# A GATv2 layer on one core: destinations loaded as 96 rows and 15, and the last destinations of units copied on chip

## The chip, the cores and the metric

The kernel runs on one core of a Trainium2 chip. The metric is the device time of one execution in microseconds (us). Three runs of the kernel before the change took 4048.72 to 4051.7 us, with a median of 4050.42.

## What is computed

One graph layer over 12500 nodes of 128 features and 400000 edges, which are sorted by destination. After a layer norm and a ReLU, the layer attends over the incoming edges of every node (GATv2, 8 heads of 16 features), and a feed-forward block follows:

```python
h = jnp.maximum(_layernorm(x, axis=-1), 0.0)
x = x + _L0_gnn_ref(h, edge_index, edge_attr_32, ...)

# within the layer
x_l = (x @ W_l).reshape(n, H, C)
x_r = (x @ W_r).reshape(n, H, C)
e = (ea @ W_e).reshape(-1, H, C)
m = jax.nn.leaky_relu(x_l[src] + x_r[dst] + e, NEG_SLOPE)
alpha = jnp.einsum('ehc,hc->eh', m, att)
a = softmax of alpha over the edges of each dst
out = jax.ops.segment_sum(x_l[src] * a[:, :, None], dst, num_segments=n)
...
h = x + _gatv2(_ln(x, ln1_g, ln1_b), edge_index, edge_attr, ...)
ff = jax.nn.gelu(_ln(h, ln2_g, ln2_b) @ W1 + b1, approximate=False) @ W2 + b2
return h + ff
```

## The kernel before

**Two parts.** A first part (the prologue, in `tile_gnn`) works on nodes: it loads x, computes layer norms and `x_l`, and stores `x_l` rows in DRAM (`xl_dram`). Then the main loop (`window_edges`) walks over the edges in 782 pairs of units; a unit is U = 256 edges. For each pair, GpSimd (POOL) issues four indirect DMAs of 128 rows each (`gather`, line 896), which fetch `x_l[src]` into a tile `xs`. `gather` runs four pairs ahead of PE's first use, and `xs` has 12 buffers. PE then combines, scores, transposes and sums; ACT and VectorE (DVE) work between its steps. The last nodes' softmax and feed-forward follow.

**The order in the prologue is written out by hand** (`tc.manual_schedule()`): each engine, and each DMA queue, executes its part in program order. Two queues matter here: SyncE's (SP), which issues the ordinary loads and stores, and GpSimd's, which issues the indirect loads. First all loads are issued: the node tiles (`load_x`), the destinations (`load_dst`), the constants (`load_consts`). Then 35 rounds follow. In each round every stage of `node_stages` handles one group of four node tiles, later stages working on earlier groups. Within a round, raw gathers and raw stores come first, then the one-time steps of certain rounds (`weights` in round 3, `edge_constants` in 7, `from_first` in 12, `fits` in 14), then the node stages. The stage `x_l` (line 535 stores its rows on SyncE's queue) starts in round 8.

**The raw batches.** 24 of the later pairs do not gather from `xl_dram`. Their four gathers are made during the prologue, straight from x (`raw_gather`, line 270), and are stored to DRAM three rounds later on SyncE's queue (`raw_store`, line 278). The tile `raw` has five buffers, so the sixth batch's gathers can begin only when the first batch has been stored.

**The destinations.** `load_dst` fills two tiles. `dc` holds all destinations, one row of EP = RU * U = 14 * 256 = 3584 edges in each of RP = 112 partitions, with the first U + 1 of the next row repeated behind it; places without an edge hold NO_NODE. Line 290 loads rows 0 to 110 as one DMA, line 293 and line 298 what is repeated behind the rows, line 302 row 111. `lu` holds the last destination of each of the 14 units of a row; it is loaded from DRAM at a stride of 256 elements (lines 305 and 308). The last unit with edges is only partly filled; line 314 puts the destination of the last real edge in its place. `from_first` casts `dc` to float (`df`, line 389) and computes, on GpSimd (`dlb`, line 393), the distance of each destination from the first of its unit or pair; `fits` reads `lu` and checks that the units suit the windowed path, and its flag chooses between `window_edges` and a general path.

`edge_constants` (first operation that needs a loaded constant: line 358, from `we_sb`) is VectorE's work in round 7. `load_consts` stands behind `load_dst` on SyncE's queue: lines 244 to 252, with `src_sb` (1568 KB, line 251) and `first_sb` (1568 single elements, line 252) as its last.

The order of the prologue:

```python
        load_x(0, min(GN, NT))
        load_raw()
        ...
        load_dst()
        load_consts()
        ...
        for r in range(max(max(len(qs), 9) + LAST + 1, rows_at[-1] + 4)):
            for d, at in zip(raw, rows_at):
                if r == at:
                    raw_gather(d)
                if r == at + 3:
                    raw_store(d)
```

Of the kernel before, what the change touches and what calls it, by code (L numbers as in the profile page):

```python
# [32 lines left out]
NO_NODE = 1 << 20  # L33
KU = 2
U = KU * P
UP = 2
QP = 4
RU = 14
# [5 lines left out]
XW = P + H  # L44
CX = XW // H
GN = 4
SPARE = 8
AHEAD = 4
WAHEAD = 3
# [41 lines left out]
def group_range(nc, pool, v, step, n):  # L91

    below = pool.tile([P, n], F32, name=f"below{n}")
    nc.vector.tensor_scalar(below, v, float(step), None, op0=OP.is_lt)
    nc.vector.scalar_tensor_tensor(v, v, 0.0, below, op0=OP.is_ge, op1=OP.mult)


def node_groups(nt):

    first = nt % GN  # L100
    return ([(0, first)] if first else []) + [(t, GN) for t in range(first, nt, GN)]


def edges_per_node(nt, n_edges):
    return -(-n_edges // (nt * P))


def done_after(nt, n_edges):

    return [-(-(t + n) * P * edges_per_node(nt, n_edges) // U) + SPARE for t, n in node_groups(nt)]  # L110


def xr_round(t0, nt, n_edges):

    first = (t0 * P - CW) * edges_per_node(nt, n_edges) // U - SPARE
    return first // UP - WAHEAD - XR_STEPS - 1


def raw_pairs(nt, n_edges):

    n_pr = -(-n_edges // (UP * U))
    at = [xr_round(t, nt, n_edges) + XR_STEPS + 1 for t in range(GN, nt, GN)]
    return [(r + RAW_STEPS + AHEAD + 1, r) for r in at if r + RAW_STEPS + AHEAD + 2 < n_pr]


def heads_of(nc, pool, out, att_c, fh):

    nc.vector.tensor_scalar(fh, fh, 0.0, None, op0=OP.is_equal)
    of = pool.tile([P, H], F32, name="of")
    nc.vector.tensor_reduce(of, fh, AX.X, OP.max)  # L130
    nc.vector.tensor_scalar(out, of, att_c, None, op0=OP.mult)
# [3 lines left out]
def tile_gnn(  # L135
# [23 lines left out]
    nc = tc.nc  # L159
# [6 lines left out]
    NUE = -(-n_edges // U)  # L166
    NU = -(-NUE // (UP * QP)) * UP * QP
    RP = -(-NU // RU)
# [23 lines left out]
    flag = keep.tile([1, 1], I32, name="flag")  # L192
    quads = [(t, min(GN, NT - t)) for t in range(0, NT, GN)]
    VAR = 6
    roots_sb = keep.tile([P, len(quads) + VAR, 2, GN], F32, name="roots_sb")
    mean_sb = keep.tile([P, NT], F32, name="mean_sb")
# [33 lines left out]
    EP = RU * U  # L230
    rest = NCH * CE - (RP - 1) * EP
    dc = rng.tile([RP, EP + U + 1], I32, name="dc")
    lu = rng.tile([RP, RU], I32, name="lu")

    def load_weights():
        nc.scalar.dma_start(wl_sb, w_l)
        nc.scalar.dma_start(wr_sb, w_r)
        nc.scalar.dma_start(g1_c, column(ln1_g))
        nc.scalar.dma_start(b1n_c, column(ln1_b))
# [40 lines left out]
    def load_x(t0, n):  # L280
        if n > 0:
            nc.sync.dma_start(h_sb[:, t0 : t0 + n, :], x_t[:, t0 : t0 + n, :])  # L282

    def load_dst():
        nc.gpsimd.memset(dc[:, EP : EP + U + 1], NO_NODE)
        if rest < EP:
            nc.gpsimd.memset(dc[(RP - 1) // DE * DE :, rest:EP], NO_NODE)
        if RP > 1:
            over = min(EP + U + 1, NCH * CE - (RP - 2) * EP)
            nc.sync.dma_start(  # L290
                dc[0 : RP - 1, 0:EP], bass.AP(tensor=dst.tensor, offset=dst.offset, ap=[[EP, RP - 1], [1, EP]])
            )
            nc.sync.dma_start(
                dc[RP - 2 : RP - 1, EP:over],
                bass.AP(tensor=dst.tensor, offset=dst.offset + (RP - 1) * EP, ap=[[0, 1], [1, over - EP]]),
            )
            if RP > 2:
                nc.sync.dma_start(
                    dc[0 : RP - 2, EP : EP + U + 1],
                    bass.AP(tensor=dst.tensor, offset=dst.offset + EP, ap=[[EP, RP - 2], [1, U + 1]]),  # L300
                )
        nc.sync.dma_start(dc[RP - 1 : RP, 0:rest], dst[(RP - 1) * EP :].rearrange("(o e) -> o e", o=1))
        nc.gpsimd.memset(lu, NO_NODE)
        if RP > 1:
            nc.sync.dma_start(
                lu[0 : RP - 1, :], bass.AP(tensor=dst.tensor, offset=dst.offset + U - 1, ap=[[EP, RP - 1], [U, RU]])
            )
        nc.sync.dma_start(
            lu[RP - 1 : RP, 0 : rest // U],
            bass.AP(tensor=dst.tensor, offset=dst.offset + (RP - 1) * EP + U - 1, ap=[[0, 1], [U, rest // U]]),  # L310
        )

        u = NUE - 1
        nc.sync.dma_start(
            lu[u // RU : u // RU + 1, u % RU : u % RU + 1],
            bass.AP(tensor=dst.tensor, offset=dst.offset + n_edges - 1, ap=[[0, 1], [1, 1]]),
        )


    def weights():  # L320
# [5 lines left out]
        wl_f = wl_c.rearrange("p c h -> p (c h)")  # L326
        ps = once_ps.tile([P, GN * P], F32, name="w_ps")
        nc.tensor.matmul(ps[:, 0:P], mean, wl_f, start=True, stop=True)
# [27 lines left out]
    def edge_constants():  # L356
        nc.vector.tensor_copy(ident_b, ident)
        nc.vector.tensor_copy(
            wer.rearrange("p (c h) -> p c h", h=H), we_sb.rearrange("p (h c) -> p c h", c=C)
        )  # L360
        heads_of(nc, build, attbd, att_c, fh)
        nc.vector.tensor_scalar(
            negrep, attbd[:, None, :].to_broadcast([P, NW, H]), -1.0, None, op0=OP.mult
        )
        nc.vector.tensor_scalar(nh, nh, 0.0, None, op0=OP.is_equal)
        mine = build.tile([P, H], F32, name="mine")
        nc.vector.tensor_reduce(mine, nh, AX.X, OP.max)
        nc.vector.tensor_copy(diag, mine[:, None, :].to_broadcast([P, CX, H]))
        nc.vector.tensor_scalar(own, own, 0.0, None, op0=OP.is_equal)
        nc.vector.tensor_scalar(last, last, 0.0, None, op0=OP.is_equal)  # L370
        nc.vector.tensor_sub(own, last, own)
        nc.vector.tensor_scalar(farw, own, BIG, None, op0=OP.mult)
        group_range(nc, build, third, NS, CW)
        nc.vector.tensor_mul(third, third, in_order)
        nc.vector.tensor_reduce(nid, third, AX.X, OP.add)
        nc.vector.tensor_scalar(unit, unit, 0.0, None, op0=OP.max)
        nc.vector.tensor_add(nid, nid, unit)
        nc.vector.tensor_scalar(fq, fq, 0.0, None, op0=OP.is_equal)
        qm = build.tile([P, QP], F32, name="qm")
        nc.vector.tensor_reduce(qm, fq, AX.X, OP.max)  # L380
        for q in range(QP):
            nc.vector.tensor_scalar(we_z[:, q, :], wer, qm[:, q : q + 1], None, op0=OP.mult)


    df = rng.tile([RP, EP + U + 1], F32, name="df")
    bad = rng.tile([RP, 2], F32, name="bad")

    def from_first():
        nc.vector.tensor_copy(df, dc)
# [11 lines left out]
    def fits():  # L401
# [30 lines left out]
        nc.vector.tensor_mul(place, place, place)  # L432
        nc.vector.tensor_scalar(off[:, 3], place, float(SPARE**2), None, op0=OP.is_gt)
        nc.vector.tensor_mul(off, off, real[:, None, :].to_broadcast([RP, 4, RU]))
# [270 lines left out]
    with tc.manual_schedule():  # L705
        make_identity(nc, ident)
        count_up()
        for t in xls:
            nc.gpsimd.memset(t[:, :, P:], 1.0)
        load_weights()  # L710
        load_x(0, min(GN, NT))
        load_raw()
        load_x(GN, min(3 * GN, NT - GN))
        for t in range(4 * GN, NT, 14):
            load_x(t, min(14, NT - t))
        load_dst()
        load_consts()
        nc.gpsimd.memset(empty, 0.0)
        nc.gpsimd.memset(empty[:, :, C + 1 : SH], CAP)
        rows_at = [i * 5 // 4 + (3 if i >= 10 else 0) for i in range(len(raw))]  # L720
# [6 lines that stand above are left out]
            if r == 3:  # L727
                weights()
            if r == 7:
                edge_constants()  # L730
            if r == 12:
                from_first()
            if r == 14:
                fits()
            for t in slots(r - 2):
                nc.vector.reciprocal(t, t)
            for t in slots(r - 1):
                nc.scalar.activation(t, t, AF.Sqrt)
            for late, f in node_stages:
                if 0 <= r - late < len(qs):  # L740
                    f(qs[r - late], r)
            if 0 <= r - LAST < len(first_xr):
                first_xr[r - LAST](qs[0])
        clear(0)
# [952 lines left out]
```

## Time and profile before

| | us |
|---|---|
| three runs: lowest, median, highest | 4048.72, 4050.42, 4051.7 |
| the profiled execution | 4055.89 |
| its span | 4053.7 |
| busy in the span: PE | 3555.2 (88%) |
| GpSimd (POOL) | 2984.9 (74%) |
| VectorE (DVE) | 2539.5 (63%) |
| ACT | 2135.2 (53%) |
| first and last gather of line 896 begin | 186.4 and 3981.5 |

The profile names an engine, a line of the kernel, and "out<-in" by tile names. A time "idle before" is that of the engine ahead of an instruction, with what ended it. SPq and POOLq are the engines' sequencers, which issue DMAs; the time of an issue on SPq includes what the queue waits for before it can hand the DMA on. In the chain of waits, "issue" is time in which an engine waited for nothing that the profile shows. The granted clock of PE was 0.955 over the span.

### The profile page before, as it was taken

What the parts mean: (1) busy time and instruction counts of PE and PEld (TensorE: products, weight loads), DVE (VectorE), ACT (ScalarE), POOL (GpSimd) and SP (SyncE); (2) the same over time, 40 slices, a digit from 0 to 9 for tenths busy, and PEclk for the clock granted to TensorE, in tenths of its full rate; (3) what the DMA queues carried; (4) which work ended last, traced back from release to release, by engine and by line L of the source; (5) the groups of instructions that cost most, each with busy time, mean ns of one, the idle gap of its engine ahead of it and who ended that gap; (6) DMA issues with size and microseconds to landing.
All of it is one profiled execution on the core that took longest, in us unless ns stands there. A gap on an engine that the chain in (4) does not pass through costs nothing.

```text
span 4053.7 us, 65778 instructions
## 1 busy us (share of the span) xinstructions
PE 3555.2 (88%) x19254; PEld 2501.5 (62%) x19255; DVE 2539.5 (63%) x5834; ACT 2135.2 (53%) x4638; POOL 2984.9 (74%) x3156
## 2 busy tenths in 40 slices
PE   2388888998989999999999999999989999989986
PEld 2356665665666666666666666666766666666664
DVE  5656665766666666666666666666666665666654
ACT  4544444544445555565455556555555555545543
POOL 4777777777777777777777777777777777777772
PEclk6699999999999999999999999999999999999998
DMA  5668878777766666656665665656666666565562
GB/s 160 198 165 198 185 194 197 171 163 165 172 124 126 126 124 131 123 121 129 132 125 124 128 129 120 136 123 117 124 136 126 124 130 128 107 135 114 120 134 50
DMA packets 648212, 560.85 MB, mean 138 GB/s; under 512 B 386387, under 2 KB 525506, under 8 KB 647602
## 3 DMA queue, kind: packets, MB, share of 16 engines
q1 hardware_dynamic: 547266, 339.01, 33.7%
q0 software_dynamic: 100000, 217.41, 30.2%
q8 instruction: 156, 2.56, 0.3%
q14 instruction: 214, 1.75, 0.2%
q10 hardware_dynamic: 576, 0.13, 0.0%
HBM read 489.81 MB, written 66.32 MB: 137 GB/s over the span
## 4 chain that ended last, share of the span: by engine, by line
PE 40%; POOL 24%; DMA 22%; issue 13%; SPq 1%; DVE 0%; ACT 0%; POOLq 0%; DVEq 0%; ACTq 0%
POOL xs L896 22%; DMA xs<-xl_dram,src_sb 21%; PE z L942 9%; PE acc L1000 8%; PE ab L960 7%; PE pt_ps L986 4%; PE z L938 4%; PE z L941 2%; PE ab L959 2%; POOL raw L270 2%; PE acc L1233 1%; PE acc L1208 1%; DMA lu<-in_dst 1%; SPq L282 0%; DMA state<-rec 0%
## 5 line engine op out<-in xcount | busy, mean ns | idle before, releaser
L896 POOL DMA_INDIRECT xs<-xl_dram,src_sb x3029 | 2873.0, 949 | 923.2 <-issue 796.0
L978 ACT ACTIVATE p<-ab,rec 128x256 f32<-128x256 f32 x1563 | 656.8, 472 | 1056.5 <-DVE rec L967 1044.3
L1009 DVE TENSOR_TENSOR own<-acc,diag 128x272 f32<-128x272 f32 x782 | 344.1, 440 | 1068.5 <-PE acc L1000 1039.6
L938 PE MATMUL z<-ident,xs 128*128 128x128 f32 x3125 | 573.3, 283 | 353.0 <-DMA xs<-xl_dram,src_sb 318.3
L938 PEld LDWEIGHTS z<-ident,xs 128*128 128x128 f32 x3125 | 399.5, 142 | 772.3 <-DMA xs<-xl_dram,src_sb 434.5
L1000 PE MATMUL acc<-xs,pt 128*128 128x136 f32 x6250 | 874.9, 284 | 0.2 <-DVE f_yo L1247 0.2
L942 PE MATMUL z<-ea,we_z 128*128 128x512 f32 x1564 | 835.4, 617 | 0.0
L1000 PEld LDWEIGHTS acc<-xs,pt 128*128 128x128 f32 x6250 | 802.6, 195 | 0.4 <-PE pt_ps L986 0.4
L960 PE MATMUL ab<-m,negrep 128*128 128x512 f32 x1564 | 801.4, 594 | 0.0
L991 ACT COPY pt<-pt_ps 128x512 f32<-128x512 f32 x782 | 455.9, 583 | 623.3 <-PE pt_ps L986 611.5
L986 PEld LDWEIGHTS pt_ps<-ident,p 128*128 128x128 f32 x3125 | 407.8, 146 | 438.2 <-issue 386.4
L967 DVE TENSOR_REDUCE rec<-ab 128x2 f32<-128x512 f32 x781 | 540.2, 692 | 123.4 <-PE ab L960 113.2
L953 DVE TENSOR_TENSOR m<-z,zs 128x512 f32<-128x512 f32 x782 | 533.0, 682 | 115.0 <-ACT zs L948 114.7
L948 ACT ACTIVATE zs<-z 128x512 f32<-128x512 f32 x782 | 472.2, 604 | 41.4 <-DMA dlw<-dc_dram 33.6
L986 PE MATMUL pt_ps<-ident,p 128*128 128x128 f32 x3125 | 489.2, 281 | 2.2 <-ACT pt L991 1.3
L1015 DVE TENSOR_REDUCE rec<-own 128x34 f32<-128x272 f32 x782 | 340.9, 436 | 26.7
L942 PEld LDWEIGHTS z<-ea,we_z 128*128 128x128 f32 x1564 | 306.5, 196 | 32.5
L960 PEld LDWEIGHTS ab<-m,negrep 128*128 128x128 f32 x1564 | 300.6, 192 | 37.1 <-issue 1.2
L941 PE MATMUL z<-ne,xrw 128*128 128x512 bf16 x782 | 304.0, 389 | 0.2 <-DMA xs<-xl_dram,src_sb 0.2
L959 PE MATMUL ab<-ne,farw 128*128 128x512 bf16 x782 | 299.6, 383 | 0.0
L924 DVE TENSOR_SCALAR ne<-dlw,nid 112x512 bf16<-112x512 bf16 x782 | 289.8, 371 | 13.0 <-DMA dlw<-du_dram 13.0
L270 POOL DMA_INDIRECT raw<-in_x,src_raw x96 | 95.5, 995 | 71.3 <-DMA raw_dram<-raw 40.1
(198 smaller groups left out, 2235.6 us busy)
## 6 DMA issues: line engine op xcount, KB each, us to landing
dlw<-dc_dram SPq DMA_DIRECT2D x196, 384.0 KB
ea<-in_ea_t SPq DMA_DIRECT2D x196, 256.0 KB
ea_s<-in_ea_t SPq DMA_DIRECT2D x98, 512.0 KB
xs<-xl_dram,src_sb POOLq DMA_INDIRECT x3029
state<-rec SPq DMA_DIRECT2D x1563, 9.0 KB
xrw<-xs_dram SPq DMA_DIRECT2D x782, 24.0 KB
state<-empty SPq DMA_DIRECT2D x28, 504.0 KB
st<-state SPq DMA_DIRECT2D x48, 288.0 KB
```

Of the source, the lines that this page charges most:

```text
L896: nc.gpsimd.indirect_dma_start(out=xs[:, j, :], out_offset=None, in_=xl_dram, in_offset=bass.IndirectOffsetOnAxis(ap=src_sb[:, c * KP + j ...
L938: nc.tensor.matmul(z[:, j * P : (j + 1) * P], d["xs"][:, j, 0:P], ident, start=(j == 0), stop=False, is_transpose=True)
L941: nc.tensor.matmul(z[:, :e], xrw[c % NV], d["ne"][:, :e], start=False, stop=False)
L942: nc.tensor.matmul(z[:, :e], we_z[:, c % QP, :], d["ea"][:, :e], start=False, stop=True)
L948: nc.scalar.activation(d["zs"][:, :e], d["z"][:, :e], AF.Copy, scale=SLOPE)
L953: nc.vector.tensor_tensor(d["m"][:, :e], d["z"][:, :e], d["zs"][:, :e], op=OP.max)
L960: nc.tensor.matmul(ab[:, :e], negrep.rearrange("p n h -> p (n h)"), d["m"][:, :e], start=False, stop=True)
L967: nc.vector.tensor_reduce(d["rec"][:, :, CX], d["ab"].rearrange("p (u e) -> p u e", e=U), AX.X, OP.min)
L978: nc.scalar.activation(d["p"][:, us], d["ab"][:, us], AF.Exp, bias=d["rec"][:, i, CX:SH], scale=-1.0)
L986: nc.tensor.transpose(d["pt_ps"][:, js], d["p"][:, js], ident)
L991: nc.scalar.copy(d["pt"][:, :e], d["pt_ps"][:, :e])
L1000: nc.tensor.matmul(d["acc"][:, i, :], d["pt"][:, j * P : (j + 1) * P], d["xs"][:, j, :], start=(j == js[0]), stop=(j == js[-1]),)
```

## The change

The load of rows 0 to 110 of `dc` is cut into two DMAs, of rows 0 to 95 and 96 to 110. The two strided loads of `lu` and its memset are removed. A new step, `last_of_units`, copies every 256th element of `dc` into `lu` on VectorE at the start of round 8, before that round's node stages; the single-element load into `lu` is moved behind this copy, and stands on SyncE's queue in round 8, behind that round's raw store and ahead of its `x_l` store.

```diff
+NQ = 16
...
         if RP > 1:
             over = min(EP + U + 1, NCH * CE - (RP - 2) * EP)
-            nc.sync.dma_start(
-                dc[0 : RP - 1, 0:EP], bass.AP(tensor=dst.tensor, offset=dst.offset, ap=[[EP, RP - 1], [1, EP]])
-            )
+            whole = (RP - 1) // NQ * NQ
+            for a, b in ((0, whole), (whole, RP - 1)):
+                if a < b:
+                    nc.sync.dma_start(
+                        dc[a:b, 0:EP],
+                        bass.AP(tensor=dst.tensor, offset=dst.offset + a * EP, ap=[[EP, b - a], [1, EP]]),
+                    )
...
-        nc.gpsimd.memset(lu, NO_NODE)
-        if RP > 1:
-            nc.sync.dma_start(
-                lu[0 : RP - 1, :], bass.AP(tensor=dst.tensor, offset=dst.offset + U - 1, ap=[[EP, RP - 1], [U, RU]])
-            )
-        nc.sync.dma_start(
-            lu[RP - 1 : RP, 0 : rest // U],
-            bass.AP(tensor=dst.tensor, offset=dst.offset + (RP - 1) * EP + U - 1, ap=[[0, 1], [U, rest // U]]),
-        )
-
-        u = NUE - 1
-        nc.sync.dma_start(
-            lu[u // RU : u // RU + 1, u % RU : u % RU + 1],
-            bass.AP(tensor=dst.tensor, offset=dst.offset + n_edges - 1, ap=[[0, 1], [1, 1]]),
-        )
...
+    def last_of_units():
+        nc.vector.tensor_copy(lu, dc[:, U - 1 : EP : U])
+
+        u = NUE - 1
+        nc.sync.dma_start(
+            lu[u // RU : u // RU + 1, u % RU : u % RU + 1],
+            bass.AP(tensor=dst.tensor, offset=dst.offset + n_edges - 1, ap=[[0, 1], [1, 1]]),
+        )
...
             if r == 7:
                 edge_constants()
+            if r == 8:
+                last_of_units()
```

## The prediction

> **What bounds the kernel now.** I read the page first, its chain and groups, then the indirect loads of line 896, then the first 200 us by engine, then SyncE's queue.
>
> ```profile
> L896 POOL DMA_INDIRECT xs<-xl_dram,src_sb x3029 | 2873.0, 949 | 923.2 <-issue 796.0
> ```
> ```profile
> L896 POOL DMA_INDIRECT xs<-xl_dram,src_sb x3029: 940/945/1702, 186.4 to 3981.5; - x190
>   issue: 796.0, 2611
>   DMA xs<-xl_dram,src_sb: 41.8, 137
> ```
> The first line is a group of the page, the others are the answer for line 896. (2873.0 + 923.2) / 3029 = 1.253 us from one gather to the next, and 3029 x 1.253 = 3796 us is the whole stretch from 186.4 to the last gather's end at 3982.5. The idle part is 0.30 us before every gather, whoever is named as releaser (41.8 / 137 = 0.305). So GpSimd never waits for a buffer in the main loop: it sets the pace, although PE is the busiest engine (88%). PE's wait for `xs` says the same from the other side, in the waits between 400 and 3900 us:
>
> ```profile
> PE z L938 <- DMA xs<-xl_dram,src_sb: 286.6, 290, 4.2
> ```
> The 71 us after the last gather (to 4053.7) drain the pipeline and the last nodes. What brings gather 1 forward thus brings the end forward one for one. GpSimd reaches it through 96 gathers of line 270, and these did wait: GpSimd's timeline,
>
> ```profile
> 30.41 0.94 POOL L270 DMA_INDIRECT raw<-in_x,src_raw  x1 [0.30 <-issue]
> 71.47 0.94 POOL L270 DMA_INDIRECT raw<-in_x,src_raw  x1 [40.12 <-DMA raw_dram<-raw]
> ```
> `raw` has 5 buffers of 4 gathers; the 21st waits until the first buffer has been stored. That store sits in SyncE's queue, whose timeline is:
>
> ```profile
> 20.25 2.83 SPq L290 DMA_DIRECT2D dc<-in_dst  x1
> ...
> 24.38 0.97 SPq L305 DMA_DIRECT2D lu<-in_dst  x1
> 25.40 25.56 SPq L308 DMA_DIRECT2D lu<-in_dst  x1
> 52.15 0.23 SPq L314 DMA_DIRECT2D lu<-in_dst  x1
> 52.43 0.38 SPq L244 DMA_DIRECT2D cols<-in_ln_g  x1
> ...
> 54.26 0.67 SPq L245 DMA_DIRECT2D cols<-in_att  x1
> 54.97 0.59 SPq L246 DMA_DIRECT2D we_sb<-in_w_e  x1
> ...
> 58.95 10.24 SPq L278 DMA_DIRECT2D raw_dram<-raw  x5
> ```
> The queue stands in L308 for 25.56 us. Why is told by the windows (PE, PEld, DVE, ACT, POOL busy, PE clock, DMA share, GB/s):
>
> ```profile
> 15.00:25.00 10.00, 3.75 (x14) 2.17 (x13) 7.70 (x47) 7.14 (x33) 7.56 (x9) 1.00 1.13 354
> 34.00:47.00 13.00, 0.00 (x0) 0.00 (x0) 0.00 (x0) 0.00 (x0) 0.00 (x0) 0.50 0.19 81
> ```
> While `h_sb` loads, all 16 DMA engines move 354 GB/s. From 34 to 47 us only `dc` moves: 0.19 x 16 = 3 engines, 81 GB/s, with every compute engine idle. Its 111 rows go to 3 engines (111 = 3 x 37; the trace has three landing events, 47.8 to 48.7). L305's 1554 single elements lie behind them on the same three (they land at 51.7), and L308 cannot be issued until they drain. VectorE stalls on the same delay, by its timeline:
>
> ```profile
> 57.20 0.27 DVE L358 COPY wer<-we_sb 128x128 f32<-128x128 f32 x1 [30.70 <-DMA we_sb<-in_w_e]
> ```
>
> **The change part by part.**
>
> *The dc load, split.* 96 = 16 x 6 rows and 15 = 15 x 1 rows, so 16 and 15 engines, by what the landing events show: rows are shared out evenly over a divisor of their number (111 rows, 3 events; the 110 rows of L298, 11). `h_sb` still comes first: its last landing events are at 25.9 to 27.3. The 1.59 MB of 111 rows at the 354 GB/s above take 4.5 us (gathers included in that rate, as they will be). From about 26.3 to 26.5 that gives 31.0 us for the 96 rows and 31.7 for the 15 (one row takes 0.54 us in the trace). Before: 48.7.
>
> [...] By the 0.19 row it gains 17 us, because the one transfer did not have 16 engines. [...]
>
> *The three lu loads, removed.* L305, L308 and L314 occupy SyncE from 24.38 to 52.38: 28.0 us including gaps. The split adds one issue (0.45, as the neighbour L293). Constants would then start at 52.43 - 28.0 + 0.45 = 24.9.
>
> *A wait that appears next.* In the trace each SyncE DMA names the semaphore that it waits for; eight are used in turn, so each DMA first waits for the landing of the one issued eight before. Before, L308 hid this. Counting after the change: the third L244 waits for the last `h_sb` (27.3), the fourth for the 96 rows (31.0), and L245 for the 15 rows (31.7). So L245 issues at 31.7, not 24.9 + 1.8 = 26.7. From L245 to the first raw store the order of issue is unchanged: 58.95 - 54.26 = 4.7 us. First raw store: 31.7 + 4.7 = 36.4, against 58.95, 22.5 us earlier. (The other eight-back DMAs, L293, L298 and L302, are small and land before 33; what waits for them issues later.)
>
> *From first store to gather 21.* 71.47 - 58.95 = 12.5 us: `src_sb` (1.6 MB) and the 1568 elements of `first_sb` lie ahead in the rings. Neither is touched and the rings are as empty at 35 us as they were at 57. Gather 21 starts at 36.4 + 12.5 = 48.9; the wait of 40.1 shrinks to 17.6. Gain 22.5 us.
>
> *VectorE.* `we_sb` is issued at 31.7 + 0.7 = 32.4 and landed 2.2 us after its issue (54.97, 57.2): 34.6, 22.6 earlier. VectorE and GpSimd move by the same amount, so what they do to each other later is kept: the gathers that took 2.5 and 3.8 us beside the cast of `df` and L404, and the 12.3 us of `dlb`.
>
> *The lu copy and the single-element load, added in round 8.* The nearest row is L410, 112x14 from int32, 0.17 us; by that row the copy costs 0.17, and a strided read could cost 0 to 0.4. VectorE is not GpSimd's limit. The one-element load takes SyncE 0.23 us, as L314 did. It waits for the copy, with the first xl store (L535) and then all later stores behind it. The copy is VectorE's first operation of round 8, at about 64.6 - 22.6 = 42; SyncE gets there after the fifth raw store, at 69.2 - 22.5 = 46.7. So it does not wait, and the xl store behind waits for later work of the same round anyway. If SyncE did get there first, the cost is bounded by slack: the raw stores land over 10 us before GpSimd wants their buffers (store 6 is issued at 78.7, gather 41 starts at 113.0). `fits` reads `lu` in round 14, 50 us on. Taken at nothing. A further DMA also shifts the turn of the semaphores by one; the xl store then waits for `src_sb`, which landed at 69.9, i.e. 47.3: 0.5 us, inside the same slack.
>
> *The removed memset of lu* (0.10 us on GpSimd) ran before GpSimd waited 2.66 us for `src_raw`: nothing.
>
> *Sum.* 22.5 us off GpSimd's start of the main loop, carried to the end. The profiled execution took 4055.89 us (span 4053.7, 2.2 outside it): 4033.4. It stands 5.5 above the median of 4050.42; the same 22.5 off the median gives 4027.9.
>
> Bounds of the unknown terms: if the rings hold `dc` up less, or the eight-back wait bites less, up to 5.0 more (27.5); if the slower gathers beside VectorE (1.5 and 2.8 us extra) fall elsewhere, 4 more; if `dc` at 16 engines runs at 250 GB/s, L245 comes 1.9 us later; if `src_sb` and `first_sb` meet traffic that they didn't meet before, up to 2.5 less.
>
> **The rivals.**
>
> 1. *No hold from the eight-back wait.* Constants run through from 24.9, gain 27.5: 4022.9. For it: L244 to L246 issue without a visible wait before. Against: their waits were over by then, and the semaphores are named in the records. 0.13.
>
> 2. [...] 0.05.
>
> 3. *PE is the true limit,* its backlog is merely hidden by 12 buffers, and an earlier start gives no earlier end: 4050. For it: PE is busy 92 of 100 us in the loop. Against: 286.6 us of waiting for `xs`, and no gather that waits for PE. 0.04.
>
> 4. *Slower: SyncE held by the new one-element load.* In round 8 it stands ahead of every xl and raw store. If the copy came late, the raw stores would come late, and GpSimd would wait at gather 41 (113.0 before, 90.4 after). It costs something only if SyncE is held beyond about 80 us, and the change loses only if held beyond about 103 (113.0 less the 10 us that the stores behind it need); each us from there is a us on the end, 4060 if held to 113. The copy needs only `dc` (31.7) and VectorE's round 7, so it is 60 us away from that point. 0.03.
>
> **How the numbers follow.** The main case has 0.75: 4027.9, by itself 4024 to 4032. The range of 4020 to 4033 takes in rival 1 with part of the 4 us of gathers; outside stay rivals 2, 3 and 4 (0.12) and some 0.07 at both ends. A measurement of this kernel can tell about 0.2% from no change, 8.1 us, so faster means below 4042.3: main case and rival 1, 0.88. Within: rivals 2 and 3, 0.09. Slower: rival 4, 0.03.
>
> **What would show each step.** GB/s near 350 up to 31 us and no window with 3 busy engines: the split. No issue of 25 us in SyncE's queue, and a hold of some 5 us at the fourth L244: the eight-back wait (if none, rival 1). VectorE's idle time before L358 about 8 us instead of 30.7; GpSimd's before gather 21 about 17.6 instead of 40.1. First gather of line 896 at 163.9 instead of 186.4, and 1.253 us apart as before. The forecast is wrong if `dc` still lands after 45, if gather 21 waits for something new, or if the 3029 gathers start to wait for PE.

## The result, and the profile after

| | before, us | after, us |
|---|---|---|
| median of 5 runs each, one chip | 4050.84 | 4033.17 |
| lowest to highest | 4048.72 to 4053.25 | 4031.16 to 4034.54 |
| the profiled execution (span) | 4055.89 (4053.7) | 4031.16 (4029.0) |
| gather 21 of the raw batches begins | 71.47 | 53.41 |
| first gather of the main loop begins | 186.38 | 168.53 |

The ratio is 0.9956, with a 95% interval of 0.9945 to 0.9967: 17.7 us less, where 22.5 were forecast. The predicted time was 4027.9, the range 4020 to 4033; the median lies 0.2 us above the range's upper end.

Lines 244 to 252 of before are lines 245 to 253 here, line 278 is 279 and line 896 is 897. The main loop runs as it did. The first line is the page's group, the others are the answer for line 897:

```profile
L897 POOL DMA_INDIRECT xs<-xl_dram,src_sb x3029 | 2868.9, 947 | 923.3 <-issue 792.7
```
```profile
L897 POOL DMA_INDIRECT xs<-xl_dram,src_sb x3029: 940/944/1554, 168.5 to 3959.6; - x190
  issue: 792.7, 2600
  DMA xs<-xl_dram,src_sb: 43.3, 142
```

(2868.9 + 923.3) / 3029 = 1.252 us from gather to gather, and still none of them waits for a buffer. What has moved is the start, by 186.38 - 168.53 = 17.85 us. The reason is at gather 21, in GpSimd's timeline (idle time before it in brackets):

```profile
30.22 0.94 POOL L271 DMA_INDIRECT raw<-in_x,src_raw  x1 [0.30 <-issue]
...
53.41 0.94 POOL L271 DMA_INDIRECT raw<-in_x,src_raw  x1 [22.25 <-DMA raw_dram<-raw]
```

It waited 22.25 us instead of 40.12. The queue that it waits for, SyncE's timeline (start, us, line):

```profile
20.16 3.93 SPq L294 DMA_DIRECT2D dc<-in_dst  x2
...
25.52 0.51 SPq L245 DMA_DIRECT2D cols<-in_ln_b  x1
27.70 7.53 SPq L245 DMA_DIRECT2D cols<-in_b  x2
36.28 0.70 SPq L246 DMA_DIRECT2D cols<-in_att  x1
37.02 0.58 SPq L247 DMA_DIRECT2D we_sb<-in_w_e  x1
...
41.02 10.47 SPq L279 DMA_DIRECT2D raw_dram<-raw  x5
51.61 0.76 SPq L382 DMA_DIRECT2D lu<-in_dst  x1
```

The 25.56 us in which the queue stood at a `lu` load are gone. In their place it stands at the third and fourth column (27.70 to 35.23) and at `att` (36.28). What it stands for is told by the waits of SyncE between 20 and 60 us (us in total, times, longest):

```profile
SPq L245 <- DMA dc<-in_dst: 6.9, 1, 6.9
SPq L245 <- DMA h_sb<-in_x: 1.7, 1, 1.7
SPq L246 <- DMA dc<-in_dst: 1.0, 1, 1.0
```

The fourth column waits for the 96 rows, `att` for the 15: each waits for the DMA issued eight before it. The last landing events of the 96 rows are at 34.9 us and of the 15 at 36.3, where 31.0 and 31.7 were forecast. The windows show how the time goes (PE, PEld, DVE, ACT, POOL busy, PE clock, DMA share, GB/s):

```profile
15.00:25.00 10.00, 3.80 (x14) 2.23 (x13) 7.77 (x48) 7.20 (x33) 7.55 (x8) 1.00 1.14 356
25.00:31.00 6.00, 4.56 (x22) 4.26 (x20) 1.31 (x6) 6.00 (x30) 4.56 (x5) 1.00 1.10 285
31.00:36.00 5.00, 1.55 (x12) 1.36 (x12) 0.00 (x0) 0.69 (x3) 0.16 (x1) 1.00 0.92 142
```

In none of these windows are only 3 DMA engines busy: the share is 0.92 and above. But from 31 to 36 us, with the DMA engines 92% busy, they move 142 GB/s. An engine can be busy with a row and move it slowly. In the DMA records, a 14336-byte row of `dc` took 536 ns in the median before, on its three engines; here it takes 986. A 12544-byte row of `src_sb`, 128 of them, takes 469. The raw gathers beside `dc` take longer too: between 25.5 and 35.5 us their 4096-byte rows take 296 ns in the median, where they took 167 before.

### The profile page after: what moved, and what is told of

Same layout as the page of the kernel before. It is cut to its first block, busy times and chain, and to the rows that moved or that the text cites. A ratio compares the mean times of both kernels' runs of the same rounds, so it can differ in the third digit from the quotient of the medians.

```text
span 4029.0 us, 65580 instructions
## 1 busy us (share of the span) xinstructions
PE 3542.0 (88%) x19059; PEld 2507.7 (62%) x19255; DVE 2539.1 (63%) x5835; ACT 2131.2 (53%) x4638; POOL 2980.9 (74%) x3155
## 4 chain that ended last, share of the span: by engine, by line
PE 38%; POOL 25%; DMA 22%; issue 13%; SPq 1%; DVE 1%; ACT 0%; POOLq 0%; DVEq 0%; ACTq 0%
POOL xs L897 23%; DMA xs<-xl_dram,src_sb 21%; PE z L943 8%; PE acc L1001 8%; PE ab L961 7%; PE pt_ps L987 4%; PE z L939 4%; PE z L942 2%; POOL raw L271 2%; PE ab L960 1%; PE acc L1234 1%; PE acc L1209 1%; SPq L283 0%; DMA state<-rec 0%; DMA dc<-in_dst 0%
## 5 line engine op out<-in xcount | busy, mean ns | idle before, releaser
L897 POOL DMA_INDIRECT xs<-xl_dram,src_sb x3029 | 2868.9, 947 | 923.3 <-issue 792.7
L939 PE MATMUL z<-ident,xs 128*128 128x128 f32 x3125 | 562.6, 283 | 349.9 <-DMA xs<-xl_dram,src_sb 319.2
L942 PE MATMUL z<-ne,xrw 128*128 128x512 bf16 (+1 forms) x781 | 305.0, 391 | 0.2 <-issue 0.2
L960 PE MATMUL ab<-ne,farw 128*128 128x512 bf16 x588 | 225.4, 383 | 0.0
```

The lines of the kernel that those rows point to most:

```text
L897: nc.gpsimd.indirect_dma_start(out=xs[:, j, :], out_offset=None, in_=xl_dram, in_offset=bass.IndirectOffsetOnAxis(ap=src_sb[:, c * KP + j ...
L939: nc.tensor.matmul(z[:, j * P : (j + 1) * P], d["xs"][:, j, 0:P], ident, start=(j == 0), stop=False, is_transpose=True)
L942: nc.tensor.matmul(z[:, :e], xrw[c % NV], d["ne"][:, :e], start=False, stop=False)
```

## The experiments

All but the first were timed beside the kernel before on the same chip, and a ratio stands against that. "G21" is the start of gather 21 (71.47 before, 53.41 after).

### The loads alone

Why did a row take about 1 us? Three theories: the partitions that the rows go to; the gathers and other traffic beside them; the source's row pitch. This kernel computes nothing: it keeps the load of x into `h_sb` and a store of it as output, and leaves out the layer. In between it issues loads of destinations, one at a time, each waiting for a small VectorE memset behind the last (in the code: rows, first partition, elements, pitch in the source).

```diff
+        nc.sync.dma_start(*load(128, 0, 3136, 3136))
+        nc.vector.memset(t_sb[:, 0:1], 0)
+        nc.sync.dma_start(*load(96, 0, 3584, 3584))
+        nc.vector.memset(t_sb[:, 0:1], 0)
...
+        nc.sync.dma_start(*load(64, 32, 3584, 3584))
```

> This kernel computes nothing of the layer: it copies x to the output and then loads pieces of the destinations into one tile, one load at a time, nothing else running: 128 rows of 12544 B, 96 rows of 14336 B, 96 of 12544 B, 96 from partition 32 on, 112 rows, 111 rows, 64 rows at partition 0, at 32 and at 64, 32 rows, 96 rows at a source pitch of 12544 B, and 128 rows again. Disputed: why the 96 rows of dc landed at 34.9 us and not at 31.0, with rows of about 1.0 us where one row took 0.54 before the change. [...] Theory G (company): the rows were slow because raw gathers and the rest of h_sb ran beside them; alone, 96 rows need 0.54 us a row, 3.3 us and a fixed part, and the partition makes no difference. Theory S (source): the pitch of the rows in DRAM decides, and 96 rows at a pitch of 12544 B differ from those at 14336 B.

VectorE's timeline shows each load as the idle time before the memset (the loads shown are, in order, 128 rows of 12544 bytes, 96 rows, 111 rows, 64 rows at partition 0, at 32, and at 64):

```profile
56.03 0.06 DVE L177 MEMSET t_sb<- 128x1 int32 x1 [6.72 <-DMA t_sb<-in_dst]
64.11 0.06 DVE L179 MEMSET t_sb<- 128x1 int32 x1 [8.02 <-DMA t_sb<-in_dst]
...
109.75 0.06 DVE L187 MEMSET t_sb<- 128x1 int32 x1 [21.93 <-DMA t_sb<-in_dst]
116.85 0.06 DVE L189 MEMSET t_sb<- 128x1 int32 x1 [7.04 <-DMA t_sb<-in_dst]
121.91 0.06 DVE L191 MEMSET t_sb<- 128x1 int32 x1 [5.00 <-DMA t_sb<-in_dst]
129.01 0.06 DVE L193 MEMSET t_sb<- 128x1 int32 x1 [7.04 <-DMA t_sb<-in_dst]
```

The records of that one execution, first packet to last, and the median of a row (two further loads are added):

| rows, partitions | bytes a row | DMA engines | us | ns a row |
|---|---|---|---|---|
| 128 at 0 | 12544 | 16 | 5.28 | 469 |
| 96 at 0 | 14336 | 16 | 6.46 | 964 |
| 96 at 0, source pitch 12544 | 14336 | 16 | 6.33 | 948 |
| 96 at 0 | 12544 | 16 | 5.56 | 828 |
| 96 at 32 | 14336 | 16 | 6.59 | 968 |
| 112 at 0 | 14336 | 16 | 6.53 | 773 |
| 111 at 0 | 14336 | 3 | 20.52 | 535 |
| 64 at 0 | 14336 | 16 | 4.70 | 1081 |
| 64 at 64 | 14336 | 16 | 4.82 | 1057 |
| 64 at 32 | 14336 | 16 | 3.11 | 535 |
| 32 at 0 | 14336 | 16 | 2.41 | 850 |

96 rows take 964 ns a row with nothing beside them, so other traffic is not what makes the row slow. The pitch isn't either (948), nor the length of the row: 12544 bytes take 828 ns in 96 rows and 469 in 128. The same 64 rows take 1081 ns in partitions 0 to 63 and 535 in 32 to 95: the place decides, by a factor of 2.0 for a row and 1.5 for the load (4.70 and 3.11 us). In 64 to 127 they take 1057. Between 535 and 1081 lie 96 rows (964) and 112 rows (773). Why the place decides is not shown.

The slow row is not the whole delay in the kernel. From the first packet to the last landing event the 96 rows took 6.9 us alone (57.08 to 63.98) and 9.4 in the changed kernel (25.48 to 34.88). There the DMA engines are shared: of 165 us of engine time that the records of 25.5 to 35.5 us add up to, 108 are rows of `dc`, and the rest is almost all raw gathers and small loads.

### One half each: the lu copy alone, the split alone

The first keeps `dc`'s 111 rows in one load and takes `lu` by the copy; the second has the split and loads `lu` an element at a time, as before. The first edit is shown against the changed kernel (what it takes out is left away), the second against the kernel before.

```diff
...
+            nc.sync.dma_start(
+                dc[0 : RP - 1, 0:EP], bass.AP(tensor=dst.tensor, offset=dst.offset, ap=[[EP, RP - 1], [1, EP]])
+            )
```

> The lu part of the change alone; rows 0 to 110 of dc are one load again, on 3 engines. Theory W (SyncE's queue first waits for dc through the wait of each DMA for the one eight before): dc lands at 48.7, the att load is held until then, the first raw store comes at 53.4, gather 21 at about 65.8 instead of 71.5: 5.6 us less than before, about 4045. Rival (the lu loads were the whole delay): constants run through from 25, first raw store at 31.5, gather 21 at 44: 27 us less than before, about 4023.

4044.32 us, ratio 0.9983 (0.9974 to 0.9992). SyncE's queue, its longest wait between 20 and 62 us, and GpSimd:

```profile
25.20 7.16 SPq L245 DMA_DIRECT2D cols<-in_b  x2
48.77 0.70 SPq L246 DMA_DIRECT2D cols<-in_att  x1
```
```profile
SPq L246 <- DMA dc<-in_dst: 16.4, 1, 16.4
```
```profile
65.76 0.94 POOL L271 DMA_INDIRECT raw<-in_x,src_raw  x1 [34.34 <-DMA raw_dram<-raw]
```

With the `lu` loads gone from ahead of the constants, `att` is issued at 48.77, when the 111 rows have landed, and G21 gains only 5.7 us. If nothing but the `lu` loads had held the queue, it would have gained 27. So the eight-back wait is real.

```diff
-            nc.sync.dma_start(
-                dc[0 : RP - 1, 0:EP], bass.AP(tensor=dst.tensor, offset=dst.offset, ap=[[EP, RP - 1], [1, EP]])
-            )
+            whole = (RP - 1) // NQ * NQ
+            for a, b in ((0, whole), (whole, RP - 1)):
...
```

> The split of dc alone; lu is loaded an element at a time again. Theory W: the 1554 elements of lu lie behind dc on 3 engines; with dc down by 36.3 they drain by about 39, the next lu load is held until then, constants begin at about 40.5 instead of 52.4, gather 21 at about 59.5: 12 us less than before, about 4039. With the other part alone at 5.6, the two parts would add up to the 17.7 measured. Rival (the elements themselves are slow, wherever dc is): SyncE's queue stays held for over 20 us, and the time is that of the kernel before.

4039.83 us, ratio 0.9970 (0.9959 to 0.9981):

```profile
26.42 13.02 SPq L313 DMA_DIRECT2D lu<-in_dst  x1
```
```profile
60.31 0.94 POOL L271 DMA_INDIRECT raw<-in_x,src_raw  x1 [28.89 <-DMA raw_dram<-raw]
```

The `lu` load is held for 13.0 us instead of 25.6. At G21 the halves give 5.7 and 11.2 us, 16.9 in sum against 18.1 together: each takes away a stretch of the queue that the other leaves.

### Other cuts of the same load

All 112 rows fit one load here, since row 111 is a full one: 16 engines with 7 rows each.

```diff
-            whole = (RP - 1) // NQ * NQ
-            for a, b in ((0, whole), (whole, RP - 1)):
-                ...
+            nc.sync.dma_start(dc[:, 0:EP], bass.AP(tensor=dst.tensor, offset=dst.offset, ap=[[EP, RP], [1, EP]]))
...
-        nc.sync.dma_start(dc[RP - 1 : RP, 0:rest], dst[(RP - 1) * EP :].rearrange("(o e) -> o e", o=1))
```

> The changed kernel with all 112 rows of dc in one load (16 engines, 7 rows each; the load of row 111 goes). [...] Rival (the two loads one behind the other cost time because the second starts late): dc lands at 31 to 32, gather 21 at about 48.5, 5 us less than the changed kernel.

4030.18 us, ratio 0.9949 (0.9935 to 0.9962). With two DMAs fewer, the hold falls on `we_sb`, which is now the eighth behind the load of `dc`. The last line is SyncE's wait:

```profile
28.03 0.70 SPq L246 DMA_DIRECT2D cols<-in_att  x1
34.90 0.56 SPq L247 DMA_DIRECT2D we_sb<-in_w_e  x1
```
```profile
SPq L247 <- DMA dc<-in_dst: 6.1, 1, 6.1
```

G21 is at 51.48, 1.9 us before the changed kernel's, at 822 ns a row; `we_sb` is issued 2.1 us earlier (34.90 for 37.02). One load with a count that 16 divides does what the split was made for. That it does a little better is seen at G21, which in a second execution of the changed kernel came at 53.56; the two ratios cannot be told apart.

The second cut loads `dc` in three parts, of which the first puts 64 rows where a row took 535 ns in the loads alone:

```diff
-            for a, b in ((0, whole), (whole, RP - 1)):
+            for a, b in ((32, 96), (0, 32), (96, RP)):
...
```

> [...] Rival (rows are slow here because of the gathers beside them): the 64 rows land no earlier than 33, all 112 at 37 or later, and the time is that of the changed kernel or longer.

4030.80 us, ratio 0.9950 (0.9936 to 0.9964).

```profile
27.22 5.05 SPq L245 DMA_DIRECT2D cols<-in_b  x2
35.05 0.61 SPq L246 DMA_DIRECT2D cols<-in_att  x1
```

In the records the first 64 rows take 535 ns in the median, with the gathers beside them (986 in the changed kernel), so the gathers were not what slowed a row of the 96. The remaining 48 rows take 1235 ns, so the last ones land at 35.75, and G21 is at 51.99: 1.4 us before the changed kernel, and against one load of 112 rows, nothing is won. From the start of the first row to the end of the last, the 112 rows take 8.8 us here, 7.9 in one load and 10.1 in the changed kernel.

### What else stands before the first store

From the first raw store to G21 12.4 us remain. `src_sb` and the 1568 single elements of `first_sb` are issued ahead of it on SyncE's queue, at 39.76 and 40.23. Here they are issued in round 16, long before the main loop uses them.

```diff
+    def load_edges():
         nc.sync.dma_start(src_sb, src)
         nc.sync.dma_start(first_sb, bass.AP(tensor=dst.tensor, offset=dst.offset, ap=[[0, 1], [U, NU]]))
...
+            if r == 16:
+                load_edges()
```

> The changed kernel with src_sb and first_sb loaded in round 16, behind the raw stores of batches 0 to 10, not ahead of the first one. The term of the sum: 12.5 us from the first raw store's issue to gather 21, put down to these two loads. Theory: raw store 1 is issued at about 40 and lands at about 42, gather 21 at about 43 instead of 53.4. VectorE still waits for we_sb until 39.4, so GpSimd, which was 9 us behind VectorE, is now beside it. If GpSimd alone set the end, line 897 would begin at 158 and the time be 4023; if VectorE's and ACT's rounds now end last, the last xl store at about 157 to 160 sets it, and line 897 begins at 160 to 162: about 4026. Rival (the raw stores are slow themselves): gather 21 stays at 51 or later, time unchanged.

4030.34 us, ratio 0.9952 (0.9938 to 0.9965): less than expected. GpSimd's timeline, then SyncE's, and last the same two `xl` stores in the changed kernel:

```profile
44.92 0.96 POOL L273 DMA_INDIRECT raw<-in_x,src_raw  x1 [13.49 <-DMA raw_dram<-raw]
...
120.90 0.94 POOL L273 DMA_INDIRECT raw<-in_x,src_raw  x1 [9.80 <-DMA raw_dram<-raw]
```
```profile
104.92 10.29 SPq L536 DMA_DIRECT2D xl_dram<-xl  x2
115.39 0.60 SPq L281 DMA_DIRECT2D raw_dram<-raw  x1
```
```profile
105.63 3.66 SPq L534 DMA_DIRECT2D xl_dram<-xl  x2
```

The step came true: G21 is at 44.92, 8.5 us earlier. But the loads now lie before the stores of rounds 17 and 18, two xl stores stand in the queue for 10.29 us instead of 3.66, the raw store behind them is issued at 115.39 (109.47 in the changed kernel), and a later raw batch waits 9.80 us for its buffer. The main loop starts at 169.0, as in the kernel after. What is gained at one buffer wait is given back at the next.

### All of the large loads later

The constants come first, `dc` is loaded in round 5, `lu` copied in round 12, `src_sb` and `first_sb` come in round 16. (`clear_dst` holds the memsets of `load_dst`.)

```diff
-        load_dst()
+        clear_dst()
         load_consts()
...
-            if r == 8:
+            if r == 5:
+                load_dst()
+            if r == 12:
                 last_of_units()
-            if r == 12:
                 from_first()
...
+            if r == 16:
+                load_edges()
```

> Order by need: the small constants first, dc in round 5 behind the first three raw stores, the lu copy in round 12, src_sb and first_sb in round 16. The same loads as in the changed kernel, in another order of SyncE's queue. Theory (GpSimd's wait for the first raw store and VectorE's for we_sb are all that the prologue loses): we_sb lands at about 27, VectorE's wait of 13.0 falls to about 1; the first raw store lands at about 31, gather 21 starts at about 32; line 897 begins at about 147 instead of 168.5, and the time is about 4012. If dc is now late for from_first in round 12 (needed at about 51), VectorE waits there and the gain is less. Rival (the prologue has another limit, such as the DMA engines, just behind): line 897 begins no earlier than about 160.

4020.09 us, ratio 0.9925 (0.9912 to 0.9939).

```profile
33.08 0.94 POOL L273 DMA_INDIRECT raw<-in_x,src_raw  x1 [1.56 <-DMA raw_dram<-raw]
...
109.27 0.94 POOL L273 DMA_INDIRECT raw<-in_x,src_raw  x1 [7.18 <-DMA raw_dram<-raw]
```

G21 hardly waits now, 38 us earlier than before. Of this 29 us arrive at the main loop, which starts at 157.3, where 147 was expected: again later batches wait, one for 7.18 us and one, earlier, for 2.22.

### Eight raw buffers

If the waits for stores of `raw` give the gain back, more buffers should keep it. The edit is one number, on the last version and on the changed kernel:

```diff
-name="raw", bufs=5
+name="raw", bufs=8
```

The first pair ran on a chip on which the kernel before takes 4852.67 us.

> The order by need of the last experiment, with 8 raw buffers instead of 5. There the start of line 897 came at 157.3 and not at 147, after two new waits of GpSimd for raw stores (7.2 us at gather 61, 2.2 at gather 30). Theory (a raw store is issued in its round on SyncE's queue, which keeps VectorE's pace, so five buffers let GpSimd run only so far ahead): both waits go; GpSimd would be done at 148, the last xl store is issued at about 147 and lands at about 149.5; line 897 begins at about 150, the time is about 4013. Rival (the rounds on VectorE and ACT end last, buffers or not): line 897 stays at 155 or later, 4018 or more.

4849.41 us, ratio 0.9990 (0.9981 to 0.9999).

> The changed kernel with 8 raw buffers instead of 5 and nothing else. GpSimd's wait moves from gather 21 to gather 33 and falls from 22.3 us to about 7 (46.4 to about 53.4). If GpSimd alone set the start of the main loop, line 897 would begin at about 153 instead of 168.5; the last xl store of the changed kernel is issued at 158.0, so I expect about 161, 7 us less than the changed kernel: about 4026. If the start of the main loop follows GpSimd's first long wait alone: 4018. If a later wait gives all of it back, as with the edges loaded late: 4033.

4841.52 us, ratio 0.9982 (0.9969 to 0.9995). Neither tests the theory, since GpSimd does not set the pace there. Of the first of them, the line of the page, and from the answer for line 904 the head and some of the idle time by what ended it:

```profile
L904 POOL DMA_INDIRECT xs<-xl_dram,src_sb x3029 | 2872.8, 948 | 1685.1 <-issue 792.8
```
```profile
L904 POOL DMA_INDIRECT xs<-xl_dram,src_sb x3029: 942/947/1707, 207.0 to 4763.8; - x190
...
  remote: 399.3, 180
  PE acc L1008: 228.8, 94
```

GpSimd idles 1685 us, where it was 923 in the changed kernel above. 229 of them end on PE's `acc`, and 399 on a release that the profile cannot place ("remote"). An earlier start should then be worth less, but how early the kernel before starts on this chip is not on record. Why this chip runs the kernel 20% longer, at a granted clock of 0.917 against 0.955, stays open: for the changed kernel with 8 buffers, the profiled spans on this chip and on the one below differ by 819 us, and PE's busy time by 256 (3810 and 3554).

On a chip where the kernel before takes 4051.68, the changed kernel was run again beside both:

> The changed kernel unedited, as the measure for the next two runs on the same chip: about 18 us less than before (4033), if the chip takes 4050 for the kernel before. On the chip of the last two runs, where the kernel before took 4853 and GpSimd did wait in the main loop, an earlier start of the loop should be worth less than one for one.

4031.66 us, ratio 0.9950 (0.9937 to 0.9964).

> As e9 on a chip that takes 4050 for the kernel before: 8 raw buffers alone. GpSimd's wait moves to gather 33 and falls to about 7 us; line 897 begins at about 161 (the last xl store, issued at 158.0 in the changed kernel, then sets it), time about 4026. If a later wait gives it back: 4033.

4020.22 us, ratio 0.9921 (0.9908 to 0.9935), 6 us less than expected. G21 waits no more, the wait is found at gather 33 and is shorter, and the main loop starts 11 us before the changed kernel's (157.8):

```profile
55.65 0.94 POOL L271 DMA_INDIRECT raw<-in_x,src_raw  x1 [9.15 <-DMA raw_dram<-raw]
```

> As e8 on a chip that takes 4050 for the kernel before: the order by need and 8 raw buffers. Theory: the waits of 7.2 and 2.2 us for raw stores go, line 897 begins at about 150, time about 4013, 20 us less than the changed kernel and 7 less than with 5 buffers (4020). Rival (the rounds on VectorE and ACT end last): line 897 at 155 or later, 4018 or more.

4013.00 us, ratio 0.9907 (0.9892 to 0.9922), the fastest version of this study: 38.7 us less than before, 18.7 less than the changed kernel on the same chip.

```profile
149.73 0.95 POOL L904 DMA_INDIRECT xs<-xl_dram,src_sb  x1 [0.15 <-POOL xrw L883]
```
## Why the prediction was right and wrong

**GpSimd's start is carried to the end one for one: right.** Over all the kernels that ran where GpSimd sets the pace, the gain at the first gather of the main loop, against 186.38, and the gain of the medians agree within 3 us. In eight of the ten the median gains more than the start; why is not known.

| kernel | start earlier, us | median lower, us |
|---|---|---|
| lu copy alone | 5.7 | 6.9 |
| split alone | 10.3 | 11.4 |
| the change (first and second time) | 17.9, 17.9 | 17.7, 20.0 |
| 112 rows in one load | 19.1 | 21.0 |
| 64, 32 and 16 rows | 19.4 | 19.4 |
| edges late | 17.4 | 19.9 |
| the change, 8 raw buffers | 28.6 | 31.5 |
| destinations late | 29.1 | 30.1 |
| destinations late, 8 raw buffers | 36.7 | 38.7 |

The two profiled spans differ by more, 24.7 us: 17.9 at the start, 4.0 in the 3029 periods (1.2533 and 1.2520 us), 2.8 behind the last gather. The profiled execution of before lies above all five of its timed runs, so this surplus is put down to that execution.

**The split gives the load its engines: right.** The stretch of 3 engines at 81 GB/s is gone, and with the `lu` copy left out the split alone is worth 11 us.

**The eight-back wait: right,** at the fourth column and at `att`, and shown by the half without the split, where `att` is held to 48.77.

**When `dc` lands: the step that failed.** The sum had "the 1.59 MB of 111 rows at the 354 GB/s above take 4.5 us", hence 31.0 and 31.7. They took about 10 us, from 26 to 36.3, the last landing event, and `att` was issued at 36.28. The rate of `h_sb`, 128 partitions, was taken for a load of 96, on the ground that both have 16 engines. The prediction's own reserve, 250 GB/s with 1.9 us, was too small as well. The loads alone show most of why: a 12544-byte row took 828 ns into the first 96 partitions and 469 into 128. In the changed kernel's records the 112 rows of `dc` took 108 us of engine time, where 112 x 0.535 = 60 would have done; over 16 engines this is an estimated 3.0 us. Where the rest of the miss comes from stays open; that the rows of the raw gathers took 296 ns instead of 167 may be a part of it. The miss is 36.3 - 31.7 = 4.6 us, and everything behind is late by 4.6: the first store 41.02 for 36.4, gather 21 at 53.41 for 48.9, the main loop at 168.5 for 163.9. 4027.9 + 4.6 = 4032.5; the medians were 4033.17 and, on another chip, 4031.66.

**From the first store to gather 21: right,** 53.41 - 41.02 = 12.4 for 12.5. The experiment with the late edges shows that `src_sb` and `first_sb` make most of it: without them ahead it took 44.92 - 40.93 = 4.0.

**VectorE: late by the same term.** Idle before its first use of `we_sb`, 13.0 for 8:

```profile
39.38 0.27 DVE L348 COPY wer<-we_sb 128x128 f32<-128x128 f32 x1 [13.00 <-DMA we_sb<-in_w_e]
```

**The lu copy and load, taken at nothing: right.** The copy starts at 46.8 and takes 0.175 us; the load is issued at 51.61 in 0.76 us (0.23 was expected) with a wait of some 0.8 for VectorE, and no gather waits for what is behind it.

**The 0.19 row: right on the engines.** By it the split was to bring `dc` down at 31.7 instead of 48.7, 17 us earlier. Measured, 36.3, 12.4 us earlier: in the loads alone 96 rows had 16 engines and 111 rows 3. One transfer did as well with a count that 16 divides: 112 rows in one load, also on 16 engines, brought gather 21 another 1.9 us forward.

**The rivals.** No hold (4022.9): refuted by SyncE's waits. A load that keeps its three engines (0.05): refuted; the `lu` copy alone, with the 111 rows in one load, took 4044.32. PE as the limit: refuted by the table above on its chips; on the slower chip GpSimd does wait for PE. Slower by a held one-element load: it did not occur; its wait of 4.3 us was seen in the kernel with the late edges, where SyncE comes to round 8 earlier, and no gather there waited for it.

## What to carry to other kernels

Before a bandwidth is carried from one load to another, compare which partitions they fill, not only how many DMA engines they have: a busy share near 1 with few GB/s was the sign of it here (0.92 and 142 from 31 to 36 us, 1.14 and 356 while `h_sb` loaded). Choose a row count that 16 divides (alone, 112 rows took 6.53 us on 16 engines, 111 rows 20.52 on 3), and keep large loads that are not yet needed behind the small ones that start the pipeline (here that brought gather 21 from 53.41 to 33.08). A wait removed at one buffer is kept only if the next buffer's store is early too (the late edges won 8.5 us at gather 21 and none at the main loop); the pair of late loads and more buffers gave about twice the gain of the edit that was studied (38.7 us, where the edit gave 20.0 on the same chip).

## What was not expected of the hardware

The prediction had no term for this: in these loads the time of a row depended on the partitions that the whole load fills. The 64 rows of 14336 bytes took 3.11 us in partitions 32 to 95, and 4.70 and 4.82 in 0 to 63 and 64 to 127, with 16 engines each time. 32 rows in partitions 0 to 31 took 2.41, about half the time of 64 there, at 850 ns a row for 1081. And the same kernel before took 4853 us on one chip and 4050 to 4052 on others.
